# Second spectral layer: ways back through DRAM tiles of their own, one reload moved ahead of the last store, unread products moved

## The chip, the core and the metric

The kernel runs on one core of one Trainium2 chip. TensorE (PE) multiplies, VectorE (DVE), ScalarE (ACT) and GpSimd (POOL) work on the results, and transfers are issued on the queues of SyncE (SP) and of ACT. The metric is device time in microseconds (us), the median of several runs. Lower is better.

## What is computed

Four layers follow each other on one image of 48 x 48 pixels with 768 channels: a transformer block, a spectral layer, a scan with a convolution, and a second spectral layer. Only the spectral layers (the second and the fourth of these) are touched. In short:

```
xs  = rfft2(x)                          # 48 x 25 modes, 768 channels
xs  = xs in 8 blocks of 96 channels
o1  = relu(xs @ w1 + b1)                # complex, per block
o2  = o1 @ w2 + b2                      # complex, per block
out = irfft2(softshrink(o2, 0.01)) + x
```

All of it is float32.

## The kernel before

The Fourier transform over the width is made first, row by row, and its result is kept in two DRAM tensors `yu[0]` and `yu[1]`, one for each half of the 768 channels, laid out as [row of the spectrum, pixel row, 384 channels]. `spectrum_mix` (L1598) then does the rest of the spectral work. It is called once for each spectral layer, as "f1" and as "f3". The profile cuts these names to `f`, so `f_x` is the tile `x_...` of either layer and `f_yt` a loaded piece of spectrum. Which layer a row belongs to is seen from its time: f1 starts near 2615 us, f3 near 3341 us.

**The pipeline of `spectrum_mix`.** Its items are (group of channel blocks, chunk of five columns of the spectrum, block). In f3 there are four groups of two blocks, five chunks and so 40 items; the loop makes 44 steps. In each step four stages work on four different items: `s_ifft_h` on the item four steps back (product `f_u`, L1682, then the sum `f_us` on DVE, L1684), `s_mlp2` on the one three steps back (products `f_z`, L1666 and L1667, then `f_cl` and `f_Z` on DVE), `s_mlp1` on the one before (products `f_o`, L1645 to L1647), and `s_fft_h` on the newest (product `f_x`, L1631, copied by ACT to `f_X` and summed by POOL to `f_Xs`). All products take their PSUM banks in turn from one pool of eight. `beside(step)` adds other work to a step.

**Unread products.** `keep_warm` (L128) makes products that nothing reads, in a fixed place of PE's order. `spectrum_mix` makes three ahead of its first step and two ahead of each of steps 1 and 2, all in one bank taken as `first` (L1693 to L1698; `f_first` in the profile). Twelve more stand at the very end of f3 (`f_warm`, L1922). One such product is two passes of 384 columns.

**The ways back in f3** (`afno_second`, L1824). When both blocks of a chunk of a group are through, `put` (L1875) stores `us` to the same columns of `yu` from which it was loaded (L1877, 360 KB). The rows come back as `gts[group]`, a tile of 128 partitions: spectrum rows on partitions 0 to 49 for one half of the pixel rows and on 64 to 113 for the other half. For groups 0 to 2 this is done in six reloads of 50 rows by eight pixel rows, after the last chunk's store (L1882). For the last group each chunk of ten rows is reloaded by itself in two transfers of 180 KB, one for each half: chunks 0, 1 and 2 right behind their own stores, chunk 3 (the last but one) together with chunk 4 after the store of chunk 4. All of the last group's transfers are kept in program order. They are on SP's queue, but for one half of chunk 4, which is on ACT's queue. A reload must wait until the store of its chunk has landed, and SP's queue waits with it.

**The end.** `back` (L1900) makes the transform back over the width (product `f_w`, L1906), adds it to `x` on ACT and DVE in turn (L64, L66), and stores the output in pieces of 144 or 288 KB (L1896). For groups 0 to 2 it runs beside later steps; for the last group it runs after the twelve unread products.

The lines that decide the order of the last group's transfers:

```
elif group == final and kc != NKC - 2:
    for k in (kc,) if kc < NKC - 1 else (kc - 1, kc):
        for b in range(2):
            reload(nc.scalar if k == NKC - 1 and b else nc.sync, b, chunk(k), 0, G // 2)
```

Of the kernel before, what the change touches and what calls it, by code (L numbers as in the profile page):

```python
# [12 lines left out]
F32 = mybir.dt.float32  # L13
# [5 lines left out]
DRAM = bass.MemoryType.DRAM  # L19

P = 128
G = 48
# [4 lines left out]
NH, HD = 12, 64  # L27
# [16 lines left out]
NB, BS = 8, 96  # L44
KW = G // 2 + 1
KC = 5
KR = 2 * KW
NKC = KW // KC
# [79 lines left out]
def keep_warm(tc, ps, left, right, n):  # L128


    k, m = left.shape
    for _ in range(n):
        tc.keep_in_program_order(tc.nc.tensor.matmul(ps[:m, : right.shape[1]], lhsT=left, rhs=right, start=True, stop=True))
# [1428 lines left out]
def spectrum_open(tc, stack, name, a, layer, yu, side, groups, bufs):  # L1562


    nc = tc.nc
    w1, b1, w2, b2 = (a[f"{layer}_{k}"] for k in ("w1", "b1", "w2", "b2"))
    cp, yp = (stack.enter_context(tc.tile_pool(name=f"{name}_{n}", bufs=bufs, side=side)) for n, bufs in (("c", 1), ("y", bufs)))
    fh = cp.tile([BS, BS], F32, tag="fh", name=f"{name}_fh")
    nc.sync.dma_start(fh, a["fh"])
    w1t = cp.tile([BS, NB, 2, BS], F32, tag="w1", name=f"{name}_w1")  # L1570
    w1s, w1d = (cp.tile([BS, NB, BS], F32, tag=n, name=f"{name}_{n}") for n in ("w1s", "w1d"))
    w2t = cp.tile([BS + 1, NB, 2, BS], F32, tag="w2", name=f"{name}_w2")
    b1t = cp.tile([BS, 2, NB], F32, tag="b1", name=f"{name}_b1")
    ih = cp.tile([BS, BS], F32, tag="ih", name=f"{name}_ih")
    nc.sync.dma_start(w1t, w1)
    nc.sync.dma_start(b1t, b1)
    nc.sync.dma_start(w2t[:BS], w2)
    nc.sync.dma_start(w2t[BS : BS + 1], b2)
    nc.sync.dma_start(ih, a["ih"])
    nc.gpsimd.tensor_tensor(w1s, w1t[:, :, 0, :], w1t[:, :, 1, :], ALU.add)  # L1580
    nc.gpsimd.tensor_tensor(w1d, w1t[:, :, 1, :], w1t[:, :, 0, :], ALU.subtract)
    yts = {}

    def load(group, kc):
        if (group, kc) not in yts:
# [12 lines left out]
def spectrum_mix(tc, name, opened, psum, side, groups, put, beside):  # L1598

# [6 lines left out]
    nc = tc.nc  # L1606
    HB = NB // 2
    (fh, w1t, w1s, w1d, w2t, b1t, ih), load = opened
    with tc.tile_pool(name=f"{name}_s", bufs=2, side=side) as sp:
# [83 lines left out]
        warm = psum("first")  # L1693
        unread = lambda n: keep_warm(tc, warm, fh, w1t[:, :2].rearrange("p n r c -> p (n r c)"), n)
        unread(3)
        for step in range(len(items) + 4):
            if 0 < step < 3:
# [126 lines left out]
def afno_second(tc, a, scan, yu):  # L1824

    nc = tc.nc  # L1830
    ev = Evac(nc)
    out = a["out"].rearrange("(p s w) c -> s w p c", s=2, w=G)
    x3, scan_psum = next(scan)
    with ExitStack() as stack:
        GB = 2
        groups = [(n * GB // (NB // 2), n * GB % (NB // 2), GB) for n in range(NB // GB)]
        opened = spectrum_open(tc, stack, "f3", a, "L3", yu, "right", groups, 5)
        gp = stack.enter_context(tc.tile_pool(name="f3_g", bufs=1, side="right"))
        fw = by_rows(nc, gp, a["fw"], G, "fw")
        iw = by_rows(nc, gp, a["iw"], KR, "iw")  # L1840
        ready = [(half, g) for half in range(2) for g in range(NTB)]

        def rows_in(n, psum):
            half, g = ready[n]
            spectrum_rows(nc, fw, x3[:, 4 * g : 4 * g + 4, half * TB : (half + 1) * TB], yu, half, g, psum, gp, ev, "f3")
            if NTB <= n < NTB + 4:
                opened[1](0, n - NTB)


        for n, _ in enumerate(scan):  # L1850
            if n and n % 2 == 0:
# [10 lines left out]
        W = GB * BS  # L1862
        x3p = x3.rearrange("p (j b) c -> p b j c", b=2)

        def channels(group):
            half, b0, _ = groups[group]
            return slice(half * TB + b0 * BS, half * TB + b0 * BS + W)

        final = len(groups) - 1

        def put(group, kc, us, cols):
            half, b0, _ = groups[group]
            if cols.stop < W:
                return
            cs = slice(b0 * BS, b0 * BS + W)  # L1875
            pin = tc.keep_in_program_order if group == final else lambda ins: ins
            pin(nc.sync.dma_start(spectrum_of(yu[half], kc, cs), us))  # L1877
            if kc == 0:
                gts[group] = bp.tile([P, G // 2, W], F32, tag="gt", name=f"f3_gt_{group}")

            def reload(queue, b, rows, r0, n):
                pin(queue.dma_start(gts[group][b * HD + rows.start : b * HD + rows.stop, r0 : r0 + n], yu[half][rows, b * (G // 2) + r0 : b * (G // 2) + r0 + n, cs]))  # L1882

            chunk = lambda k: slice(2 * KC * k, 2 * KC * (k + 1))
            if group < final and kc == NKC - 1:
                for r0 in range(0, G // 2, 8):
                    for b in range(2):
                        reload(nc.sync, b, slice(0, KR), r0, 8)
            elif group == final and kc != NKC - 2:
                for k in (kc,) if kc < NKC - 1 else (kc - 1, kc):  # L1890
                    for b in range(2):
                        reload(nc.scalar if k == NKC - 1 and b else nc.sync, b, chunk(k), 0, G // 2)

        def store(queue, prs, cols):
            for s in range(2):
                queue.dma_start(out[s, :, prs, cols], x3[s * HD : s * HD + G, prs, cols])  # L1896

        def back(group, c):
            cols = channels(group)
            gt = gts[group].rearrange("p (j s) c -> p s j c", s=2)  # L1900
            for j in range(2):
                ps = [psum(f"w_{group}_{c}_{j}_{b}") for b in range(2)]
                for b in range(2):
                    keep = slice(b * HD, b * HD + KR)
                    for s in range(2):
                        nc.tensor.matmul(ps[b][s * HD : (s + 1) * HD, : 2 * W], lhsT=iw[keep], rhs=gt[keep, s, 4 * c + 2 * j : 4 * c + 2 * j + 2, :], start=True, stop=True)  # L1906
                for b in range(2):
                    ev(x3p[:, b, 4 * c + 2 * j : 4 * c + 2 * j + 2, cols], ps[b][: HD + G, : 2 * W].rearrange("p (j c) -> p j c", j=2))
                if group == len(groups) - 1:
                    store((nc.scalar, nc.sync)[j], slice(8 * c + 4 * j, 8 * c + 4 * j + 4), cols)  # L1910
            if group < len(groups) - 1:
                store(nc.scalar, slice(8 * c, 8 * c + 8), cols)

        each = NKC * GB
        backs = {each * (q + 1) + 8 + (2 if q < final - 1 else 1) * c: (q, c) for q in range(final) for c in range(3)}

        def beside(step):
            if step in backs:
                back(*backs[step])

        spectrum_mix(tc, "f3", opened, psum, "left", groups, put, beside)
# [111 lines left out]
```

## Time and profile before

| what | us |
|---|---|
| median of 3 runs | 3575.01 (3571.93 to 3576.77) |
| the profiled execution: its own time | 3578.66 |
| its span | 3576.8 |
| PE busy | 3513.7 (98%) |
| DVE, ACT, POOL busy | 2004.7, 1141.4, 680.8 |
| f_first: PE passes in the whole program, and longest | 28 of up to 0.53 |
| the 20 stores of `us` in f3, 360 KB each | issued from 3363 to 3551 |

The chain of waits is the work that ended last, followed back from the last instruction: what each piece waited for, or the piece before it on its engine. A line gives its start, its length and what it was. "issue" is time in which the engine waited for nothing that the profile shows. In lines of a timeline, the bracket at the end tells how long the engine stood idle before and what ended this. "SPq" and "ACTq" are the instructions that issue transfers on the queues of SP and ACT; merged lines include the waits between them. `f_gt<-yu` is a reload, `yu<-f_us` a store of a chunk, `f_yt<-yu` the load of a chunk, `out_dram<-x` a store of the output. In a table of stretches the columns are: length, busy time and instructions of PE, of the weight loads, of DVE, ACT and POOL, the clock granted to TensorE, the mean busy share of 16 DMA engines, and GB/s.

### The profile page before, as it was taken

Reading aid. Unit: us, or ns where it says so; the run is one execution under the profiler, and the core shown is the slowest. Engines: PE = TensorE matmul, PEld = TensorE weight load, DVE = VectorE, ACT = ScalarE, POOL = GpSimd, SP = SyncE. Lnnn points to the kernel's source line nnn. Section 1 sums busy time; section 2 is a strip of 40 time slices with the busy share of each in tenths; the row PEclk is TensorE's granted clock in tenths of the full one; section 3 lists DMA queues with packets and bytes.
Section 4 is the critical chain, followed back from the end, with each engine's and each line's share of the span. In section 5 each row is a group of like instructions: output and inputs, shape, how many; then the busy total and the mean of one; then the engine's idle time right before and its main releaser. Section 6 shows DMA issues by size and latency. Waiting matters only on the chain.

```text
span 3576.8 us, 52953 instructions
## 1 busy us (share of the span) xinstructions
PE 3513.7 (98%) x21274; PEld 2148.0 (60%) x21274; DVE 2004.7 (56%) x3015; ACT 1141.4 (32%) x1735; POOL 680.8 (19%) x572
## 2 busy tenths in 40 slices
PE   9999999999999999989999999999999998999998
PEld 5666554444444444555555555555578767996685
DVE  7644466766676776654234324232345578996554
ACT  1321254555555555203101210121023265223332
POOL 3211102111111110250000000000023303981121
PEclk9999999999999999999999999999999999999999
DMA  7555556655545443344346334533554403104456
GB/s 276 201 187 189 187 156 173 187 145 152 164 123 148 125 125 87 111 150 139 106 131 184 114 110 126 164 112 112 156 134 119 109 21 105 34 27 100 107 143 132
DMA packets 281171, 480.38 MB, mean 134 GB/s; under 512 B 37250, under 2 KB 234466, under 8 KB 274708
## 3 DMA queue, kind: packets, MB, share of 16 engines
q1 hardware_dynamic: 265322, 455.95, 43.8%
q10 hardware_dynamic: 15594, 20.94, 2.0%
q8 instruction: 171, 2.80, 0.3%
q14 instruction: 84, 0.69, 0.1%
HBM read 330.82 MB, written 145.98 MB: 133 GB/s over the span
## 4 chain that ended last, share of the span: by engine, by line
PE 91%; DVE 3%; POOL 2%; DMA 2%; ACT 1%; issue 1%; SPq 0%; ACTq 0%; DVEq 0%; POOLq 0%
PE p L996 14%; PE p L1059 13%; PE s L657 12%; PE av L688 12%; PE qk L375 6%; PE c L1223 4%; PE s L667 3%; PE c L1323 3%; PE v L180 3%; PE pj L180 3%; PE f_u L1682 2%; PE f_z L1666 2%; PE f_z L1667 2%; PE so L1410 2%; PE f_x L1631 2%; POOL t L1331 1%
## 5 line engine op out<-in xcount | busy, mean ns | idle before, releaser
L677 DVE TENSOR_TENSOR acc<-acc,p 128x928 f32<-128x928 f32 (+1 forms) x480 | 560.2, 1167 | 263.6 <-ACT p L669 222.6
L669 ACT ACTIVATE p<-s 128x928 f32<-128x928 f32 (+1 forms) x540 | 506.5, 940 | 491.6 <-PE s L667 470.0
L657 PE MATMUL s<-qt,kv 64*128 64x464 f32 (+1 forms) x2160 | 521.9, 559 | 7.5 <-DMA qt<-q_d 5.5
L1059 PE MATMUL p<-w,h 128*128 128x384 f32 x1512 | 492.3, 486 | 0.0
L688 PE MATMUL av<-p,kv 128*64 128x464 f32 (+1 forms) x2160 | 442.9, 554 | 0.0
L1059 PEld LDWEIGHTS p<-w,h 128*128 128x128 f32 x1512 | 285.6, 190 | 199.0 <-issue 4.2
L667 PE MATMUL s<-bt,oneh 64*128 64x464 f32 (+1 forms) x1080 | 400.8, 731 | 0.7 <-DMA bt<-rh_d 0.7
L688 PEld LDWEIGHTS av<-p,kv 128*64 128x64 f32 x2160 | 147.0, 137 | 261.9 <-issue 249.6
L657 PEld LDWEIGHTS s<-qt,kv 64*128 64x128 f32 x2160 | 203.0, 187 | 164.7 <-issue 153.4
L996 PE MATMUL p<-x2nT,w 128*128 128x384 f32 x864 | 294.0, 491 | 4.0 <-POOL rr L1035 4.0
L1323 PE MATMUL c<-H,bands 128*48 128x96 f32 x5632 | 245.1, 247 | 10.2 <-DVE th L1261 8.3
L375 PE MATMUL qk<-xnT,wqk 128*128 128x384 f32 x756 | 249.8, 487 | 0.3 <-DMA wqk<-wqk_d 0.3
L1323 PEld LDWEIGHTS c<-H,bands 128*48 128x48 f32 x5632 | 235.2, 124 | 20.3 <-issue 8.7
L996 PEld LDWEIGHTS p<-x2nT,w 128*128 128x128 f32 x864 | 165.2, 192 | 121.3 <-POOL rr L1035 4.2
L996 PE MATMUL p<-xT,w 128*128 128x384 f32 x648 | 220.8, 486 | 0.0
L1035 POOL TENSOR_TENSOR rr<-rr,ml_b 128x1152 f32<-128x1152 f32 x12 | 31.8, 2653 | 946.1 <-DMA rr<-xr_d 855.1
L991 ACT ACTIVATE h<-h,ml_b 128x384 f32<-128x384 f32 x144 | 88.5, 616 | 346.7 <-DVE h L1011 173.5
L375 PEld LDWEIGHTS qk<-xnT,wqk 128*128 128x128 f32 x756 | 141.4, 190 | 93.4 <-issue 0.9
L1331 POOL TENSOR_TENSOR t<-s,c 128x768 f32<-128x768 f32 x80 | 144.4, 1829 | 179.4 <-DVE s L1294 166.5
L996 PEld LDWEIGHTS p<-xT,w 128*128 128x128 f32 x648 | 123.1, 190 | 85.9
L667 PEld LDWEIGHTS s<-bt,oneh 64*128 64x128 f32 x1080 | 106.9, 188 | 105.7 <-issue 102.9
L1666 PE MATMUL f_z<-f_w,f_o 97*96 97x96 f32 x800 | 134.1, 249 | 0.0
(336 smaller groups left out, 4601.2 us busy)
## 6 DMA issues: line engine op xcount, KB each, us to landing
w<-w1s_d SPq DMA_DIRECT2D x36, 768.0 KB
w<-w2s_d SPq DMA_DIRECT2D x36, 768.0 KB
w<-w1s_d SPq DMA_DIRECT2D x36, 576.0 KB
w<-in_mlp_w_dram SPq DMA_DIRECT2D x27, 768.0 KB
yu<-f_ys SPq DMA_DIRECT2D x48, 384.0 KB
wqk<-wqk_d SPq DMA_DIRECT2D x12, 1344.0 KB
bt<-rw_d SPq DMA_DIRECT2D x72, 174.0 KB
bt<-rh_d SPq DMA_DIRECT2D x72, 174.0 KB
```

The lines of the kernel that those rows point to most:

```text
L180: nc.tensor.matmul(p[:, :TB], lhsT=rhs[n][:, c, t * P : (t + 1) * P], rhs=w[:, c, :], start=c == 0, stop=c == NC2 - 1)
L375: nc.tensor.matmul(p[:, :TB], lhsT=w[:, n, c, :], rhs=ops[sb][n][:, c, :], start=c == 0, stop=c == NC2 - 1)
L657: nc.tensor.matmul(ps[:, s, :n], lhsT=keys[pr % 2][rows, kt * P : (kt + 1) * P], rhs=held(c)[rows, :n], start=True, stop=False)
L667: nc.tensor.matmul(ps[:, s, :n], lhsT=oneh[rows, b % 2, :], rhs=bts[b // 2][rows, j, :n], start=False, stop=True)
L669: nc.scalar.activation(p, ps[:, :, :n], AF.Exp)
L677: nc.vector.tensor_tensor(probs[c], probs[c], p, ALU.add)
L688: nc.tensor.matmul(avs[c][rows, : size(c)], lhsT=vals[pr % 2][:, kt, rows], rhs=p[:, s, :], start=kt == 0, stop=kt == NT - 1)
L996: nc.tensor.matmul(p[:, :TB], lhsT=w[n][:, c, :], rhs=rhs[n][:, c, :], start=c == 0, stop=c == NC2 - 1)
L1059: nc.tensor.matmul(ps[t][:, :TB], lhsT=hs[left, f][:, t * P : (t + 1) * P], rhs=wt[:, f % KW2, :], start=f == 0, stop=f == NF2 - 1)
L1323: nc.tensor.matmul(ps[r0 : r0 + G, k // 4, cols], lhsT=bands[:, n - GC, i, :] if gr else bands0[:, n, i, :], rhs=H[:, n, :, d : d + NPR], ...
L1331: GP.tensor_tensor(t, sc[:, ch], c1[:, m0 : m0 + GC].unsqueeze(2).to_broadcast([P, GC, RR, NPR]), ALU.mult)
L1666: nc.tensor.matmul(out, lhsT=o1[:, j, 1:3, :].rearrange("c r h -> c (r h)"), rhs=w2t[:, b, 0, :], start=True, stop=False)
```

## The change

- The last stage of f3 gets DRAM tiles of its own, one for each group: [50 rows of the spectrum, 48 pixel rows, 192 channels]. `put` stores a chunk there and reloads it from there, and no longer goes through `yu`. In such a tile the pixel rows of one spectrum row, with all their channels, are one run of memory.
- For the last group every chunk is reloaded right behind its own store. Chunk 3 (the last but one) is therefore reloaded ahead of the store of chunk 4 on SP's queue.
- `spectrum_mix` no longer makes three unread products ahead of the first step, in either layer. In f3, which passes `alone=True`, it makes two ahead of each of the last two steps, 42 and 43. Each batch takes a bank of its own from the pool.

```
--- before.py
+++ after.py
@@ -1595,7 +1595,7 @@
     return yu[2 * KC * kc : 2 * KC * (kc + 1), :, cols].rearrange("(k r) p c -> (r p) k c", r=2)
 
 
-def spectrum_mix(tc, name, opened, psum, side, groups, put, beside):
+def spectrum_mix(tc, name, opened, psum, side, groups, put, beside, alone=False):
 
 
 
@@ -1690,11 +1690,9 @@
         items = [(g, kc, b) for g, (_, _, n) in enumerate(groups) for kc in range(NKC) for b in range(n)]
 
         stages = {s_ifft_h: 4, s_mlp2: 3, s_mlp1: 1, s_fft_h: 0}
-        warm = psum("first")
-        unread = lambda n: keep_warm(tc, warm, fh, w1t[:, :2].rearrange("p n r c -> p (n r c)"), n)
-        unread(3)
+        unread = lambda n: keep_warm(tc, psum(f"unread_{step}"), fh, w1t[:, :2].rearrange("p n r c -> p (n r c)"), n)
         for step in range(len(items) + 4):
-            if 0 < step < 3:
+            if 0 < step < 3 or alone and step > len(items) + 1:
                 unread(2)
             for stage, behind in stages.items():
                 if 0 <= step - behind < len(items):
@@ -1860,6 +1858,8 @@
 
         gts = {}
         W = GB * BS
+        dp = stack.enter_context(tc.tile_pool(name="f3_d", bufs=1, space=DRAM))
+        backs_d = [dp.tile([KR, G, W], F32, tag=f"yb{n}", name=f"yb{n}") for n in range(len(groups))]
         x3p = x3.rearrange("p (j b) c -> p b j c", b=2)
 
         def channels(group):
@@ -1869,27 +1869,24 @@
         final = len(groups) - 1
 
         def put(group, kc, us, cols):
-            half, b0, _ = groups[group]
             if cols.stop < W:
                 return
-            cs = slice(b0 * BS, b0 * BS + W)
             pin = tc.keep_in_program_order if group == final else lambda ins: ins
-            pin(nc.sync.dma_start(spectrum_of(yu[half], kc, cs), us))
+            pin(nc.sync.dma_start(spectrum_of(backs_d[group], kc, slice(0, W)), us))
             if kc == 0:
                 gts[group] = bp.tile([P, G // 2, W], F32, tag="gt", name=f"f3_gt_{group}")
 
             def reload(queue, b, rows, r0, n):
-                pin(queue.dma_start(gts[group][b * HD + rows.start : b * HD + rows.stop, r0 : r0 + n], yu[half][rows, b * (G // 2) + r0 : b * (G // 2) + r0 + n, cs]))
+                pin(queue.dma_start(gts[group][b * HD + rows.start : b * HD + rows.stop, r0 : r0 + n], backs_d[group][rows, b * (G // 2) + r0 : b * (G // 2) + r0 + n, :]))
 
             chunk = lambda k: slice(2 * KC * k, 2 * KC * (k + 1))
             if group < final and kc == NKC - 1:
                 for r0 in range(0, G // 2, 8):
                     for b in range(2):
                         reload(nc.sync, b, slice(0, KR), r0, 8)
-            elif group == final and kc != NKC - 2:
-                for k in (kc,) if kc < NKC - 1 else (kc - 1, kc):
-                    for b in range(2):
-                        reload(nc.scalar if k == NKC - 1 and b else nc.sync, b, chunk(k), 0, G // 2)
+            elif group == final:
+                for b in range(2):
+                    reload(nc.scalar if kc == NKC - 1 and b else nc.sync, b, chunk(kc), 0, G // 2)
 
         def store(queue, prs, cols):
             for s in range(2):
@@ -1918,7 +1915,7 @@
             if step in backs:
                 back(*backs[step])
 
-        spectrum_mix(tc, "f3", opened, psum, "left", groups, put, beside)
+        spectrum_mix(tc, "f3", opened, psum, "left", groups, put, beside, True)
         keep_warm(tc, psum("warm"), opened[0][0], opened[0][1][:, :2].rearrange("p n r c -> p (n r c)"), 12)
         for c in range(3):
             back(final, c)
```

More of the change, by code (lines that the diff above doesn't have):

```diff
@@ L1595, in spectrum_of, with spectrum_mix @@
     return yu[2 * KC * kc : 2 * KC * (kc + 1), :, cols].rearrange("(k r) p c -> (r p) k c", r=2)
-def spectrum_mix(tc, name, opened, psum, side, groups, put, beside):
+def spectrum_mix(tc, name, opened, psum, side, groups, put, beside, alone=False):
     nc = tc.nc
@@ L1692, in spectrum_mix @@
         stages = {s_ifft_h: 4, s_mlp2: 3, s_mlp1: 1, s_fft_h: 0}
-        warm = psum("first")
-        unread = lambda n: keep_warm(tc, warm, fh, w1t[:, :2].rearrange("p n r c -> p (n r c)"), n)
-        unread(3)
+        unread = lambda n: keep_warm(tc, psum(f"unread_{step}"), fh, w1t[:, :2].rearrange("p n r c -> p (n r c)"), n)
         for step in range(len(items) + 4):
-            if 0 < step < 3:
+            if 0 < step < 3 or alone and step > len(items) + 1:
                 unread(2)
@@ L1862, in afno_second @@
         W = GB * BS
+        dp = stack.enter_context(tc.tile_pool(name="f3_d", bufs=1, space=DRAM))
+        backs_d = [dp.tile([KR, G, W], F32, tag=f"yb{n}", name=f"yb{n}") for n in range(len(groups))]
         x3p = x3.rearrange("p (j b) c -> p b j c", b=2)
@@ L1871, in put @@
         def put(group, kc, us, cols):
-            half, b0, _ = groups[group]
             if cols.stop < W:
                 return
-            cs = slice(b0 * BS, b0 * BS + W)
             pin = tc.keep_in_program_order if group == final else lambda ins: ins
-            pin(nc.sync.dma_start(spectrum_of(yu[half], kc, cs), us))
+            pin(nc.sync.dma_start(spectrum_of(backs_d[group], kc, slice(0, W)), us))
             if kc == 0:
@@ L1881, in reload @@
             def reload(queue, b, rows, r0, n):
-                pin(queue.dma_start(gts[group][b * HD + rows.start : b * HD + rows.stop, r0 : r0 + n], yu[half][rows, b * (G // 2) + r0 : b * (G // 2) + r0 + n, cs]))
+                pin(queue.dma_start(gts[group][b * HD + rows.start : b * HD + rows.stop, r0 : r0 + n], backs_d[group][rows, b * (G // 2) + r0 : b * (G // 2) + r0 + n, :]))
             chunk = lambda k: slice(2 * KC * k, 2 * KC * (k + 1))
@@ L1888, in put @@
                         reload(nc.sync, b, slice(0, KR), r0, 8)
[L1889 to L1892, printed above, removed]
+            elif group == final:
+                for b in range(2):
+                    reload(nc.scalar if kc == NKC - 1 and b else nc.sync, b, chunk(kc), 0, G // 2)
         def store(queue, prs, cols):
@@ L1919, in beside @@
                 back(*backs[step])
-        spectrum_mix(tc, "f3", opened, psum, "left", groups, put, beside)
+        spectrum_mix(tc, "f3", opened, psum, "left", groups, put, beside, True)
         keep_warm(tc, psum("warm"), opened[0][0], opened[0][1][:, :2].rearrange("p n r c -> p (n r c)"), 12)
```

## The prediction

> **What bounds the kernel now.** I read the page's first part, then the chain of waits over the last 240 us and the last 40 us, SP's queue in the same time, and the table of 1 us stretches.
>
> TensorE (PE) is nearly always busy. From 3357 to 3542 us the chain of the second spectral layer is PE alone, in steps of 4.57 us (6.2 with a way back in them), so what is changed beside those steps costs nothing. Only where PE waits can the change pay. The stage's start:
>
> ```profile
> PE 3513.7 (98%) x21274; PEld 2148.0 (60%) x21274; DVE 2004.7 (56%) x3015; ACT 1141.4 (32%) x1735; POOL 680.8 (19%) x572
> ...
> 3339.97 1.27 issue
> 3341.24 2.15 PE f_first L133 x6
> 3343.39 0.86 PE f_x L1631 x10
> ```
>
> Three unread products (six passes) stand between the wait for a bank and the first real product, f_x. The first spectral layer starts likewise:
>
> ```profile
> 2615.24 2.15 PE L133 MATMUL f_first<-f_w,f_fh 96*96 96x384 f32 x6 [0.74 <-DVE rr L1039]
> 2617.22 1.01 PE L1631 MATMUL f_x<-f_fh,f_yt 96*96 96x96 f32 x10
> ```
>
> The end:
>
> ```profile
> 3543.88 1.25 PE f_u L1682 x2
> 3545.13 0.32 PE f_z L1666 x2
> ...
> 3550.72 0.67 DVE f_us L1684
> ...
> 3551.40 3.70 DMA yu<-f_us
> ...
> 3555.12 7.88 DMA f_gt<-yu
> ...
> 3563.25 6.99 PE f_w L1906 x46
> ```
>
> A store, a reload and the products back follow each other with nothing beside them. A pair of f_z passes takes 0.32 us where all steps before show 0.17: the clock is halved. The stretches (last three columns: clock, DMA share, GB/s) say so too, and show a reload at 91 GB/s, the last stores at 262:
>
> ```profile
> 3545.00:3546.00 1.00, 1.00 (x8) 1.00 (x7) 0.00 (x0) 0.00 (x0) 0.00 (x0) 0.50 1.10 200
> 3559.00:3560.00 1.00, 0.00 (x0) 0.00 (x0) 0.00 (x0) 0.00 (x0) 0.00 (x0) 1.00 0.75 91
> 3573.00:3574.00 1.00, 0.00 (x0) 0.00 (x0) 0.00 (x0) 0.00 (x0) 0.00 (x0) 0.50 0.90 262
> ```
>
> SP's queue (chunks of the final group counted 0 to 4): chunk 2 is reloaded at 3540.28, chunk 3 stored at 3541.37, chunk 4 at 3551.40, and only then come the reloads of 3 and 4:
>
> ```profile
> 3540.28 0.69 SPq L1882 DMA_DIRECT2D f_gt<-yu  x2
> 3541.37 10.34 SPq L1877 DMA_DIRECT2D yu<-f_us  x2
> 3551.80 3.59 SPq L1882 DMA_DIRECT2D f_gt<-yu  x3
> ```
>
> The landing events give the ends: store 3 at 3548.07; reload of chunk 3, half 0, at 3557.84, half 1 at 3560.29; of chunk 4 at 3563.00 and 3563.70.
>
> [...] the last three halves landed 2.45 and 2.71 us apart (chunks 0 to 2: 1.9 to 2.1). [...] the trace shows ten separate landing events for such a reload, sixteen for a store. [...] it is 0.50 from 3544.8 to 3548.2 after a wait of 1.53 us; after the wait of 1.43 at 3548.2 it is not.
>
> **The change, part by part** (own time of the profiled execution 3578.66, span 3576.8).
>
> *Three unread products less, second layer.* f_x waits for the same bank and its data landed long ago: it moves from its start at 3343.22 to f_first's, 3341.24. Gain 2.0. Nothing else comes late: the first product's copies need ACT and POOL, which are idle.
>
> *The same, first layer.* There f_x needs its first load, whose last landing event is at 2616.55, not 2617.22: 0.6 at most. But PE then waits from 2614.5 to 2616.6, 2.1 us; if the clock halves, f_x (0.85) and what it overlaps run at half speed, and the first f_o, which stands at 2619.69, starts at about 2616.6 + 1.7 + 1.7 (copy and sum) + 0.3 = 2620.3, a loss of 0.6. I take 0; both ends go into the range.
>
> *A bank of its own per batch of unread products.* The eight-bank ring is moved by one; the readers of the reused banks were done over 1.5 us before. 0.
>
> *Two products ahead of each of the last two f_u.* Four passes of 0.32 us are 1.3 us, inside the waits of 1.53 and 1.43. They hold the clock: f_z's last batch takes 1.87 instead of 3.30 us, f_u a little less, so us is complete 1.6 us earlier, and the store of chunk 4 can start at 3549.8. Cost if the cover were gone: 2.6.
>
> *Contiguous DRAM tiles.* Stores keep runs of 768 B. Reloads of groups 0 to 2 (50 rows) get runs of 6144 B, of the final group 18,432 B. Such runs do get joined: the layer's way-in stores show packets of 6144 B. This shortens the 5.9 us in which SP issues six reloads, beside PE's steps: 0 on the path. For the final group it changes the packets[...]: I take 2.71 us a half as before. Bounds: nothing, or 1.4 us a half (a packet of 18,432 B elsewhere took 0.71, two per engine) if packets are the limit.
>
> *Chunk 3 reloaded ahead of store 4.* On SP the store of chunk 4 is now queued behind the wait for store 3 (3548.07) and two issues (0.7): free at 3548.9, before 3549.8, so the wait itself costs 0. Store 3 may land a little earlier, as the whole of SP's queue moved up: I take 3547 (bounds 3545 and 3549.7). But on the ten engines the packets of reload 3 now stand ahead of store 4's. That order is in the trace: the reload of chunk 0 was issued at 3521.77, its halves landed at 3526.97 and 3529.10, and store 1, queued behind it, at 3529.64: 7.9 us after the reload's issue. Store 4 then lands at 3547.1 + 7.9 = 3555.0, against 3555.1 now. Next the reload of chunk 4, alone: 1.0 us to the first packet (as from 3551.40 to 3552.4), two halves one after the other at 2.5 each, 0.3 to land: 6.3, so 3561.3, against 3563.70. Gain 2.4. It contains the 1.6 above: us is early, but the queue is late next. If halves 0 and 1, on SP's and ACT's queues[...], run side by side, 2.5 more.
>
> *The products back* still start about 4 us after the 24 warm passes end (3558.4 - 1.6), so the clock is halved again, and the last stores run at 220 to 260 GB/s whatever comes before: 0. If the reload landed within a microsecond of the warm passes, 48 passes would take 4.4 instead of 7 us, and the stores start some 1.1 us earlier.
>
> Sum: 2.0 + 0 + 2.4 = 4.4 us, so 3574.3 beside 3578.66. The runs' median, 3575.01, lies 3.65 below the profiled execution; [...] some of them need not have the halved f_z (1.6), and there the gain is smaller. I take 0.4 off: 4.0, **3571.0 us**.
>
> **Rivals.**
> *A. Packets[...] bind the reload, or its two halves overlap.* Reload 4 takes 3.8 us or less, store 4 lands near 3553.5, the last half at 3557.5, and the products run partly at full clock: 6.2 + 1.1 + 2.0 = 9.3, less 0.4: 3566. For: the tiles' rows become one run; two queues. Against: 50-row reloads of the same 768 B packets move at up to 211 GB/s, and reload halves stood 2.7 apart[...].
> *B. Only the start pays.* Store 4 stands so long behind reload 3 (landing at 3557, halves of 2.71) that reload 4 is no earlier: gain 2, 3573.
> *C. Slower: SP is held ahead of store 3.* Before store 2, SP waited 4.2 us for an output store to land, though its data was ready. If other transfers now fall together so, ahead of store 3 (3541.4), until the outputs of 3540.85 land (3549.7), store 3 lands at 3553, store 4 and reload 4 follow 8.0 + 6.3 later at 3567.3: 3.6 lost against 2.0 won, with the 0.6 in the first layer 2.2 net, 3577.2. It decides once store 3 lands after 3551.4 (3563.7 + 2.0 - 14.3).
> *D. No joined runs:* packets stay 768 B; the order and the start still act, as forecast, and so it is inside the forecast's case.
>
> **Numbers.** Forecast 0.5 (own range 3568 to 3573.5), A 0.27, B 0.16, C 0.07. The range reaches to A's and past B's time: 3564.5 to 3575.5, leaving out some of A below and C above. 0.2% of 3575 is 7.15 us, about what a measurement can tell: faster means below 3567.9. A's most and the forecast's lower edge: 0.29; C beyond 3582: 0.03; the rest 0.68.
>
> **What would show it.** f_first gone and f_x at 3341.2 less what came before; f_z pairs at 0.17 to the end; reload packets of 18,432 B; the last store's landing 3 to 7 us after its issue; reload halves 2.5 us apart or together. I'm wrong if they land together, or if store 3 lands much before 3545 or after 3551.

## The result, and the profile after

The changed kernel took 3568.58 us in the median of 12 runs (3565.89 to 3575.88), the kernel before 3575.21 us (12 runs, 3571.93 to 3579.33). The ratio is 0.9984, 95% interval 0.9976 to 0.9992: a gain of 2.9 to 8.6 us. The forecast was 3571.0 us.

Together with these, the three sets of runs below hold 54 runs of the changed kernel and 165 of the kernel before. Their means are 3570.21 and 3575.25 us. The standard deviations, divided by the root of the number of runs, make these means uncertain by 0.5 and 0.2. So the change is worth **5.0 us, give or take 0.5**. The forecast's sum was 4.4, less 0.4: 4.0.

The two profiled executions differ by 12.7 us in span (3576.8 and 3564.1), more than the change is worth (the one after was the fastest of its twelve runs), so the first question is where. From marks that both traces have ("third f_o" is the first f_o product of the third item):

| stretch | before, us | after, us | gain |
|---|---|---|---|
| start to the last MLP product ahead of the first spectral layer | 2614.50 | 2607.11 | 7.4 |
| from there to the third f_o of that layer | 14.23 | 13.70 | 0.5 |
| from there to the last way-in product of the second | 710.7 | 710.9 | -0.1 |
| from there to the second layer's third f_o | 15.21 | 14.55 | 0.7 |
| from there to the last f_x | 177.21 | 177.21 | 0 |
| from the last f_x to the end | 44.93 | 40.65 | 4.3 |

The first line stands ahead of everything that the diff touches, so it is not the change's; the same mark moved by up to 7.6 us over the profiles of all kernels here, which share that code. What the change did is in the lines below it.

What answers to the lines shown of before is, first, the chain at the second spectral layer's start (start, length, what):

```profile
3332.21 1.27 issue
3333.48 1.06 PE f_x L1631 x10
3334.54 2.17 PE f_unread L133 x4
3336.71 0.80 PE f_o L1645 x2
```

The three products are gone and f_x follows the wait for a bank. But the four passes of unread products now take 2.17 us, where six took 2.15 before, and f_x 1.06 against 0.86. One stretch of 1 us shows why (last columns: clock, DMA share, GB/s):

```profile
3336.00:3337.00 1.00, 1.00 (x4) 0.60 (x3) 0.00 (x0) 0.00 (x0) 0.00 (x0) 0.50 0.98 252
```

The clock is halved there, from 3334.8 to 3338.2 us, 3.4 us long; before it was 1.00 at this place (3341 to 3346). The first layer's start, on PE's timeline:

```profile
2604.69 2.42 PE L1059 MATMUL p<-w,h 128*128 128x384 f32 x7
2609.28 1.06 PE L1631 MATMUL f_x<-f_fh,f_yt 96*96 96x96 f32 x10 [2.17 <-DMA f_yt<-yu]
2611.79 0.65 PE L1645 MATMUL f_o<-f_Xs,f_w 96*96 96x240 f32 x2 [0.16 <-POOL f_Xs L1635]
```

PE waits 2.17 us for the load, as the forecast said, and this time keeps its clock (1.00 from 2607 to 2613). The chain of the end:

```profile
3538.00 0.18 PE f_z L1667 x2
...
3539.60 1.06 PE f_u L1682 x2
...
3540.68 0.67 DVE f_us L1684
...
3541.37 3.93 DMA yb<-f_us
...
3545.36 6.21 DMA f_gt<-yb
...
3551.71 4.10 PE f_w L1903 x44
```

f_z pairs stay at 0.17 us up to the last, the last store leaves 1.6 us earlier (17.92 us after the last f_x began, 19.53 before), its landing takes about as long as before (3.93 and 3.70), the reload 6.21 instead of 7.88, and the products back 4.10 instead of 6.99. SP's queue in that time:

```profile
3532.95 0.32 SPq L1875 DMA_DIRECT2D yb<-f_us  x1
3538.40 0.65 SPq L1880 DMA_DIRECT2D f_gt<-yb  x2
3541.37 0.32 SPq L1875 DMA_DIRECT2D yb<-f_us  x1
3545.32 0.27 SPq L1880 DMA_DIRECT2D f_gt<-yb  x1
3554.65 5.56 SPq L1893 DMA_DIRECT2D out_dram<-x  x6
```

Store 3, reload 3, store 4, reload 4: the new order. SP was free 2.3 us ahead of store 4. And the queues' totals in packets (then MB and share):

```profile
q1 hardware_dynamic: 256952, 455.95, 43.4%
q10 hardware_dynamic: 15364, 20.94, 2.0%
```

On q1 8370 packets are gone, on q10 230, with the same bytes. 18 reloads of groups 0 to 2 fell from 400 packets to 50 each (6300), ten of the final group from 240 to 10 each (2300, one of them on ACT's queue): together 8600, every one. The runs of memory are joined into longer packets, as forecast.

### The profile page after: what moved, and what is told of

The parts are those of the page before. It is cut to its first block, busy times and chain, and to the rows that moved or that the text cites. A ratio compares the mean times of both kernels' runs of the same rounds, so it can differ in the third digit from the quotient of the medians.

```text
span 3564.1 us, 52947 instructions
## 1 busy us (share of the span) xinstructions
PE 3507.8 (98%) x21270; PEld 2145.7 (60%) x21270; DVE 2002.1 (56%) x3015; ACT 1140.5 (32%) x1735; POOL 677.3 (19%) x572
## 4 chain that ended last, share of the span: by engine, by line
PE 90%; DVE 4%; DMA 3%; POOL 2%; ACT 1%; issue 1%; SPq 0%; ACTq 0%; DVEq 0%; POOLq 0%
PE p L996 14%; PE p L1059 13%; PE s L657 12%; PE av L688 12%; PE qk L375 6%; PE c L1223 4%; PE s L667 3%; PE c L1323 3%; PE v L180 3%; PE pj L180 2%; PE f_u L1682 2%; PE f_z L1667 2%; PE f_z L1666 2%; PE so L1410 2%; PE f_x L1631 2%; PE f_o L1645 1%
```

## The experiments

All times in the next table are from the start of the last f_x. S is the landing of a chunk's store (its last landing event), R3 and R4 are the reloads of chunks 3 and 4 (second half's landing), "tail" is the time to the span's end.

| kernel | S3 | R3 issued | S4 | R4 | tail |
|---|---|---|---|---|---|
| before | 17.29 | 19.93 | 23.23 | 31.83 | 44.93 |
| after | 14.94 | 14.95 | 21.85 | 28.13 | 40.65 |
| after, second (e8) | 15.77 | 15.79 | 22.83 | 29.11 | 42.19 |
| after, third (e11) | 16.55 | 16.57 | 23.48 | 29.71 | 42.61 |
| e1, shared `yu` | 16.97 | 16.99 | 24.15 | 29.95 | 42.95 |
| e2, old order | 15.83 | 18.34 | 21.43 | 29.51 | 42.70 |
| e3, no end products | 18.50 | 18.51 | 25.53 | 31.78 | 44.82 |
| e4, e10, tail only | 16.13, 16.49 | 16.15, 16.51 | 22.99, 23.55 | 29.31, 30.03 | 42.45, 42.74 |
| e5, rows spread | 14.49 | 14.51 | 20.85 | 25.60 | 38.36 |
| e6, products back in the first layer | 15.98 | 16.00 | 22.85 | 29.37 | 42.34 |
| e7, products back in the second layer | 17.13 | 17.14 | 23.90 | 30.12 | 43.04 |
| e9, start only | 18.88 | 19.93 | 22.89 | 31.84 | 45.09 |

Theory 1 is the forecast's: order pays, the last reload keeps its time whatever the length of its packets, tiles and end products are worth nothing. Each experiment names its rival. Each time below stands beside the kernel before of its own set (3575.45 us for e1 to e4, 3574.55 for e5 to e8, 3575.91 for e9 to e11); means are compared with 3575.25 and 3570.21, and "±" gives one standard error. The kernel before itself averaged 3575.5, 3574.6 and 3575.9 in the three sets, and the changed kernel did not run in the first of them, so differences of about 1 us between kernels of different sets are not read.

### e1: the tiles undone

The order and the products stay, and the ways back go through `yu` again.

```
+            half, b0, _ = groups[group]
+            cs = slice(b0 * BS, b0 * BS + W)
...
-            pin(nc.sync.dma_start(spectrum_of(backs_d[group], kc, slice(0, W)), us))
+            pin(nc.sync.dma_start(spectrum_of(yu[half], kc, cs), us))
...
-                pin(queue.dma_start(gts[group][b * HD + rows.start : b * HD + rows.stop, r0 : r0 + n], backs_d[group][rows, b * (G // 2) + r0 : b * (G // 2) + r0 + n, :]))
+                pin(queue.dma_start(gts[group][b * HD + rows.start : b * HD + rows.stop, r0 : r0 + n], yu[half][rows, b * (G // 2) + r0 : b * (G // 2) + r0 + n, cs]))
```

> The changed kernel, but stores and reloads go through the shared yu again (runs of 768 B), with the new order and the products at the end kept. The measure is the tail, from the start of the last forward product f_x to the end of the span: 44.9 us before, 40.7 after; and the last reload of chunk 4, from its issue to its second landing: 7.9 us before, 6.2 after. Theory 1 ([...] the tiles add nothing on the path): reload 6.0 to 6.6, tail 40 to 41.5. Rival (the long runs of the own tiles made the reload quicker): reload 7 to 8, tail 42.5 to 44, and most of the gain in time gone.

Measured: 3572.18 us, ratio 0.9990 (0.9982 to 0.9998). With packets of 768 B the last reload took 5.80 us from S4 to R4, against 6.28 with packets of 18,432 B in the changed kernel. Long runs do not speed it. Its halves landed 0.67 us apart, with long runs 1.79 (1.4 to 2.0 in every kernel with long runs and ten neighbouring rows). In the changed kernel each half was ten packets, and each packet of the second half (begun from 3547.11 to 3548.67) began where one of the first ended (from 3547.10 to 3548.67). The tail, 42.95, is longer than theory 1 wanted and lies where the rival had it, though not by the rival's way: the reload was not slower, but S3 landed at 16.97, just above what the changed kernel shows by itself in three profiles (14.94 to 16.55). The mean, 3571.51, is 1.3 ± 1.0 above the changed kernel's.

The tiles do move something ahead of S3. SP's queue at the six reloads of the group before and at the first store of the last group, in the kernel before and then in the changed one:

```profile
3507.05 6.10 SPq L1882 DMA_DIRECT2D f_gt<-yu  x6
3513.25 1.90 SPq L1877 DMA_DIRECT2D yu<-f_us  x1
```

```profile
3498.53 2.48 SPq L1880 DMA_DIRECT2D f_gt<-yb  x6
3501.51 0.32 SPq L1875 DMA_DIRECT2D yb<-f_us  x1
```

With tiles the six reloads take 2.48 us to issue and not 6.10, and that store goes out as soon as its data is there, 21.9 us ahead of the last f_x in all ten kernels with tiles; in the three that go through `yu` (before, e1, e9) it goes out 18.5 to 18.7 us ahead of it. The next store lands 3.7 to 6.5 us ahead of the last f_x with tiles, 2.0 to 2.7 through `yu`. S3 itself lies at 14.5 to 18.5 with tiles and at 17.0 to 18.9 through `yu`. So the tiles may have a part in the gain at the end, by way of S3; that they do is not shown.

### e2: the old order of the last two chunks

```
-            elif group == final:
-                for b in range(2):
-                    reload(nc.scalar if kc == NKC - 1 and b else nc.sync, b, chunk(kc), 0, G // 2)
+            elif group == final and kc != NKC - 2:
+                for k in (kc,) if kc < NKC - 1 else (kc - 1, kc):
+                    for b in range(2):
+                        reload(nc.scalar if k == NKC - 1 and b else nc.sync, b, chunk(k), 0, G // 2)
```

> The changed kernel, with chunk 3 reloaded behind the store of chunk 4 as before; own tiles and the products at the end kept. Theory 1: reload 4 queues behind reload 3 again, 7.5 to 8 us from the landing of store 4; the products at the end still bring store 4 forward by 1.6 us; the products back find a halved clock: tail 43 to 43.6. Rival (long runs move quickly, the order is nothing): all four halves land within 5 us of the store, tail 40 to 41.

Measured: 3569.05 us, ratio 0.9983 (0.9975 to 0.9991); mean 3569.28, not above the changed kernel's. SP's queue shows the order back:

```profile
3533.60 8.74 SPq L1875 DMA_DIRECT2D yb<-f_us  x2
3542.44 3.38 SPq L1880 DMA_DIRECT2D f_gt<-yb  x3
```

The tail, 42.70, is a little shorter than the 43 to 43.6 of theory 1. R4 lands 8.08 us after S4 (before: 8.60), because two reloads share that time; in the new order it is 6.28. Yet R4 lands at 29.51, between the changed kernel's 28.13 and 29.71. The reason is in S4. With the old order no reload stands between stores 3 and 4 on SP's queue, so the 1.6 us that the end products give reach its landing (21.43 against 23.23). With the new order S4 follows R3's issue instead: it came 6.8 to 7.2 us after it, in all kernels with ten neighbouring rows, whether store 4 was issued 0.7 or 3.0 us after it. In the changed kernel's trace the packets of reload 3 ended from 3540.16 to 3543.55, and those of store 4, issued at 3541.37, ran from 3542.21 to 3544.88. So of the 2.3 us that R4 gained here (31.83 to 29.51) 1.8 were there at S4, without the new order. This reads as if **the order and the end products were substitutes**, both together giving little more than either. It is argued from single profiles and not shown in time: no kernel here has the tiles and the shorter starts and neither of the two, and the times of e2 and e3 alone would fit as well if neither paid.

### e3: no unread products at the end

```
-        spectrum_mix(tc, "f3", opened, psum, "left", groups, put, beside, True)
+        spectrum_mix(tc, "f3", opened, psum, "left", groups, put, beside)
```

> The changed kernel without the two unread products ahead of each of steps 42 and 43. If the clock halves there, as it did in the profile of the kernel before (f_z passes at 0.16), the store of chunk 4 is issued 1.6 us later. Theory 1 (the store lands behind reload 3[...] anyway): about 1 us of it shows, tail 41.3 to 42.2. Rival (the products are the whole gain): tail 43 or more. Where the clock does not halve in this execution, the tail is that of the changed kernel, 40.7, in both.

Measured: 3568.69 us, ratio 0.9983 (0.9976 to 0.9990); mean 3569.35, again not above the changed kernel's. With the new order no worth of the end products shows in time, as the forecast had it. The profile can't tell whether a late store 4 would be hidden: the clock did not halve in it ahead of the last products, and `us` was complete at 17.89, as with the end products, and not at 19.50 as in the profiles of before and e9. Yet its tail is long, 44.82, where theory 1 had 40.7 without a halved clock, and its queue tells why:

```profile
3532.57 1.05 SPq L1880 DMA_DIRECT2D f_gt<-yb  x2
3533.72 1.00 SPq L1875 DMA_DIRECT2D yb<-f_us  x1
3541.09 0.65 SPq L1880 DMA_DIRECT2D f_gt<-yb  x2
3541.83 0.32 SPq L1875 DMA_DIRECT2D yb<-f_us  x1
3548.13 0.27 SPq L1880 DMA_DIRECT2D f_gt<-yb  x1
```

Reload 2, the first line, went out 10.0 us after the last f_x began (5.6 in the changed kernel), since store 2 landed that late; store 3 stood behind it on SP's queue, so it was issued 1.6 us later than in the changed kernel, and landed at 18.50. Store 4 was ready at 3540.5 and was held: SP issued it at 3541.83. This is the forecast's rival C, short of the point from which it costs more than it wins. One execution came that near; the 19 runs say it isn't the rule. (In e9's profile, with the old order, store 2 was as late and S3 came at 18.88.)

### e4, e6 and e7: the three first products back in both layers, in the first, in the second

```
-            if 0 < step < 3 or alone and step > len(items) + 1:
-                unread(2)
+            if step < 3 or alone and step > len(items) + 1:
+                unread(2 if step else 3)
```

This is e4. In e6 two lines are added instead, here in one: `if not step and not alone: unread(3)`; in e7 `if not step and alone: unread(3)`.

> The changed kernel with three unread products ahead of the first step again, in both layers. The measure is the time from the end of the last way-in product to the second f_o batch of the second layer: 10.7 us before, 10.1 after (where the clock was halved for 3.4 us after the wait of 1.8). Theory 1 (the three products stand on the path): 10.7 at full clock, 2.0 more than the changed kernel at full clock would need (8.7). Rival (they hold the clock and pay for themselves): the changed kernel and this one come out equal, within 0.7, because the clock halves without them. First layer, from the last product of the MLP to the first f_o: 5.2 us before, 4.7 after; here 5.2.

> The changed kernel with the three products ahead of the first step kept in the first spectral layer only. Theory 1 (the first load's landing ends the wait there anyway): 0.5 us slower than the changed kernel at the first f_o, nothing else. Rival (what is won in the first layer grows behind it): 3 us or more, which would explain the 5.7 us by which the median with both was above the changed kernel's.

> The changed kernel with the three products kept in the second spectral layer only. Theory 1: 2.0 us slower at full clock, 0.7 where the clock halves after the wait of 1.8 us; median 1 to 2 us above the changed kernel. Rival (the second layer's start is worth more than its products, since all transfers of the last group follow it): 4 us or more.

Measured: e4 3574.26 us, ratio 0.9996 (0.9987 to 1.0004); e6 3569.01, 0.9987 (0.9981 to 0.9994); e7 3570.88, 0.9990 (0.9983 to 0.9996). Means: e6 3569.99, as the changed kernel; e7 3570.89, 0.7 ± 0.6 above it. So the first layer's products are worth nothing that shows (0.6 would not show either), the second's perhaps 0.7. But e4, which only does both edits at once, stood 5.7 us above the changed kernel's first median. Two parts worth 0 and 0.7 don't make 5.7, and its trace has no place for it: its start is the one of before (15.20 us to the third f_o), its tail, 42.45, is that of the changed kernel. Hence the next two sets.

### e8 and e11: the changed kernel again

> The changed kernel once more, for a second profile and to see how far its time moves by itself. Theory 1: reload 3 is issued when store 3 has landed, store 4 lands 6.9 to 7.2 us after that issue, and the last reload 6.2 to 6.4 after store 4, so the last landing is 13.2 us after store 3's, whatever store 3's is (14.4 to 18.5 us after the last f_x so far); tail 40.6 to 43. Rival (the steps vary by themselves): the sum of 13.2 does not hold. Median 3567 to 3571.

> The changed kernel unaltered, a third time, so that the two halves above have the whole beside them on the same chip. Theory 1: 4 to 6.5 us below the kernel before. Its profile shows how far the landing of the store of chunk 3 and the clock in the products back move from one execution to the next: landing 14.4 to 18.5 us after the last forward product began, last reload 13.2 after that.

Measured: 3569.37 us, ratio 0.9986 (0.9980 to 0.9993), and 3569.84, 0.9984 (0.9978 to 0.9991). The whole is steady over three sets. What moves the end is seen in the third execution's chain:

```profile
3545.01 5.55 DMA yb<-f_us
3550.63 6.17 DMA f_gt<-yb
3556.94 7.43 PE f_w L1903 x44
```

The reload takes what it took before (6.17 and 6.21). The last store takes 5.55 us instead of 3.93, since S3 and so R3's issue came 1.6 later. And the products back take 7.43 instead of 4.10: PE had waited longer (3.29 us ahead of the first f_w, 1.64 in the changed kernel's first profile), and the clock was halved (0.50 in the stretch from 3558 to 3559).

### e9 and e10: only the start, only the end

e9 is the kernel before without one line; e10 is e4 again.

```
-        unread(3)
```

> The kernel before, without the three unread products ahead of the first step of either layer; nothing else of the change. Theory 1 (the gain is the sum of what the trace shows at its places: 0.4 to 1.0 us at the first layer's start, 0.7 to 2.0 at the second's, about 2.5 at the end): 1.1 to 3.0 us below the kernel before, so 3572 to 3574; the end as before, with the last reload landing 15 to 16 us after the landing of the store of chunk 3 and the tail near 45 us. Theory 2 (what the runs of the three-first kernel said: the end is worth 1 us and the starts the rest): 5 us or more below the kernel before.

> The changed kernel with the three unread products back ahead of the first step of both layers, so only the end of the change is left; the same kernel as the three-first one, run again. Theory 1: 2.0 to 3.0 us below the kernel before, and 1 to 3 above the changed kernel; together with the start-only kernel the two gains make up the whole. Theory 2: again no more than 1.2 below the kernel before. If the two gains sum to less than the whole change's by over 2 us, either they help each other or the medians move by that much.

Measured: e9 3575.61 us, ratio 0.9996 (0.9988 to 1.0005), mean 3574.31; e10 3573.22 us, ratio 0.9994 (0.9986 to 1.0002). With e4's runs e10's kernel has 26, mean 3573.46. So the start alone gains 0.9 ± 1.0 us and the end alone 1.8 ± 0.5 (against the kernel before of each one's own set: 1.6 ± 1.1 and 2.2 ± 0.5). e10's kernel is 3.2 ± 0.7 above the changed one, so part of e4's 5.7 was chance. The 15 to 16 us that the expectation had from store 3 to the last reload rest on a wrong landing of store 3 (see below); they were 14.5 in the kernel before and 13.0 here. Theory 2 of these two (the starts carry 5 us) falls. e10's timeline shows one thing more:

```profile
3333.39 3.20 PE L133 MATMUL f_unread<-f_w,f_fh 96*96 96x384 f32 x6 [1.78 <-issue]
3336.38 1.66 PE L1631 MATMUL f_x<-f_fh,f_yt 96*96 96x96 f32 x10
```

Here the six passes took 3.20 us and f_x 1.66, at a clock of 0.50 (the stretch from 3336 to 3337): it can be halved *with* the three products too.

### e5: the ten rows of a chunk spread over the partitions

The final group's rows go to every fifth partition instead of ten neighbours; the matrix of the transform back is loaded once more with its rows in the same order. Theory 1 is here that the reload's time hangs on the partitions on which its rows land. Its 1.4 us a half is the author's estimate, half of the 2.71 us that lie between two landings of halves in the kernel before.

```
+        iws = bp.tile([P, iw.shape[1]], F32, tag="iws", name="f3_iws", bufs=1)
+        for k in range(NKC):
+            for b in range(2):
+                nc.sync.dma_start(iws[b * HD + k : b * HD + KR : NKC], a["iw"][2 * KC * k : 2 * KC * (k + 1)])
...
-                    reload(nc.scalar if kc == NKC - 1 and b else nc.sync, b, chunk(kc), 0, G // 2)
+                    queue = nc.scalar if kc == NKC - 1 and b else nc.sync
+                    pin(queue.dma_start(gts[group][b * HD + kc : b * HD + KR : NKC], backs_d[group][chunk(kc), b * (G // 2) : (b + 1) * (G // 2), :]))
...
-                        nc.tensor.matmul(ps[b][s * HD : (s + 1) * HD, : 2 * W], lhsT=iw[keep], rhs=gt[keep, s, 4 * c + 2 * j : 4 * c + 2 * j + 2, :], start=True, stop=True)
+                        nc.tensor.matmul(ps[b][s * HD : (s + 1) * HD, : 2 * W], lhsT=(iws if group == final else iw)[keep], rhs=gt[keep, s, 4 * c + 2 * j : 4 * c + 2 * j + 2, :], start=True, stop=True)
```

> The changed kernel, but the ten rows of each chunk of the last group come back to every fifth partition and not to ten neighbours, with the rows of the last transform's matrix in the same order. [...] Theory 1[...]: two halves of 1.4 us and not of 2 to 2.7, so store 4 lands at most 5.5 us after reload 3's issue and the last reload takes 3.8 to 4.6 us and not 6.2 to 6.4; tail 38 to 39.5. Rival (packets or the ten engines bind it): reload 6 us or more, tail 40.5 to 42.5.

Measured: **3565.64 us**, ratio 0.9975 (0.9967 to 0.9984), mean 3565.67: 9 us below the kernel before and 4.5 ± 0.8 below the changed one, the best of all kernels here. The same bytes in the same packets of 18,432 B took 4.75 us from S4 to R4 instead of 6.28, R3 took 4.61 from its issue instead of 6.35, and the halves of the last reload landed 0.99 apart instead of 1.79. A packet of its second half took 2.0 us in the changed kernel and 0.9 here. So the partitions on which the rows land did bind the reload, for 1.5 of its 6.28 us. Two of the expectation's figures, the author's estimates, were missed: 4.6 for the reload by a little, and store 4, which came 6.3 us after R3's issue and not 5.5, as it was only issued 3.4 us after it. PE's timeline and SP's queue show the rest:

```profile
3538.61 7.90 PE L133 MATMUL f_warm<-f_w,f_fh 96*96 96x384 f32 x24
3546.45 4.96 PE L1908 MATMUL f_w<-f_gt,f_iws 50*64 50x384 f32 x48
```

```profile
3536.09 1.47 SPq L1894 DMA_DIRECT2D f_gt<-yb  x2
3539.50 0.31 SPq L1879 DMA_DIRECT2D yb<-f_us  x1
3542.45 0.72 SPq L1894 DMA_DIRECT2D f_gt<-yb  x1
```

The store of chunk 4 lands 2.93 us after its issue, and the products back follow the twelve warm products with no wait and a full clock (48 passes in 4.96 us, 6.98 before). The tail is 38.4 us.

## Why the prediction was right, and where it was not

**The time.** 3571.0 was forecast; 3568.58 was the first median, 3570.2 the mean of all runs, inside the forecast's own case. Rival A's time, 3566, is about as near to that first median, but its mechanism isn't what happened: the halves did not run side by side, and R4 took 6.3 us, not 3.8. Rival B needed S4 two microseconds later than before; in the three profiles of the changed kernel it came between 1.4 earlier and 0.3 later. Rival C's mechanism was seen once with the new order (e3, S3 at 18.50), short of its point: 3551.4 us in before's time is 19.5 in the table. Rival D is out by the count of packets.

**Second layer's start: 2.0 forecast.** f_x came 1.98 earlier after the last way-in product (1.79 us, before 3.77). The step had a gap: "nothing else comes late" left out the clock, which it had considered for the first layer alone. After the wait of 1.78 us it was halved in seven of the nine profiles without the products (for 3.4 us in the changed kernel's; the four unread passes took 1.94 to 2.77 us in the seven, 1.46 in e3 and e5), and there only 0.66 of the 1.98 was left at the third f_o. It is no pure loss of the change, since with the products the clock halved in two profiles of four (e7 and e10, where six passes took 2.78 and 3.20 us; 2.15 in before and e4). At equal clock the gain is what was forecast: 15.20 to 13.27 (not halved, e4 and e3), 16.85 to 14.55 (halved, e10 and after). The means over the profiles of each kind, 15.96 and 14.26, give 1.7. The clock was halved or not after the same wait of 1.78 us; what decides it is not shown. At the end of the kernel before it was 0.50 from 3544.5 to 3547.9 us, behind a wait of 1.53, and 1.00 behind the wait of 1.43 at 3548.2. That in some executions f_z is not halved there, for which the forecast took 0.4 off, was the author's estimate; e3's profile is one, with waits of 1.53 and 1.43 us.

**First layer: 0, within 0.6.** f_x does wait for its load. The third f_o came 14.2 us after the last MLP product with the three products, and 13.2 to 13.7 without, in all profiles but one: e8, where the clock halved after the wait of 2.09 us (four unread passes in 2.05 us, 1.46 in the changed kernel), had 14.92, the loss of about 0.6 that the step named. On average 0.6 is gained, the step's upper end. In time e6 is 0.2 ± 0.9 below the changed kernel, which can't show 0.6 either way.

**End products: absorbed.** Nothing speaks against it: `us` was 1.6 earlier than in the two profiles in which the clock halved without them (before, e9), and without them the new order loses no time (e3 is 0.9 ± 0.8 below the changed kernel). A late store 4 behind reload 3 was not seen. What the step did not see is that the 1.6 reach S4 in the old order (e2).

**Tiles: 0 on the path.** For the last reload this was right: its packets did not matter (6.2 to 6.5 us in eight profiles with long runs, 5.80 in e1). But the step put at nothing that SP issues the six reloads sooner, while the step on the order let store 3 land earlier because SP's queue moved up. What that is worth is open (e1, 1.3 ± 1.0).

**The order: 2.4.** The sum came out about right, in part by luck, and three of its terms were off. The landing of store 3 was misread: 3548.07 is where the first of the two output stores of 3540.85 landed. The semaphore on which SP waits ahead of reload 3 has its last landing event at 3549.16, the 17.29 of the table. So to take store 3 at 3547 meant 2.2 us earlier, not 1.1, and it came: in the changed profile it was 3546.8 (3531.87, where the last f_x began before, and 14.94), in the two others 3547.6 and 3548.4. Store 4 was to land 7.9 us after reload 3's issue; it took 6.8 to 7.2 in all kernels of the new order with neighbouring rows, so this term was 0.9 too large. The last reload was to take 6.3, and took 6.28; but of its parts 1.0 to the first packet with 2.5 a half was not right: the first half landed after 4.49 us and the second 1.79 later. Together R4 follows S3 by 13.0 to 13.5 us in every such kernel, where 14.3 was forecast. With before's own S3 of 17.29 that makes 30.3 to 30.8 against 31.83: the order by itself is worth 1.0 to 1.5 there, and the rest of what R4 gained (3.7 in the profile shown, 2.7 and 2.1 in the two others) came from S3 being earlier. In the old order R4 does not hang on S3: it was 31.83 and 31.84 with S3 at 17.29 and 18.88 (before, e9). So the order pays only as far as S3 is early; at 18.88 it would by this sum have won nothing. S3 moves between 14.5 and 18.9, and it follows the landing of store 2 by 8.0 to 9.5 us in all thirteen profiles. So what moves it lies ahead of store 2 (the six reloads, the output stores of the group before); beyond e1, that was not tried.

The reload's time was half right. The prediction took 2.71 us a half whatever the packets, which is what lay between the landings at 3560.29 and 3563.00 before, and the time did not fall with long packets. Which partitions the rows land on has a part in it, as e5 shows. Two halves of 1.36 us, half of 2.71 (the author's estimate for spread rows), would save 2.7 us; measured were 1.5 of 6.3. So where the ten rows lie cost 1.5 here. What makes up the other 4.75 is not shown.

**The products back: 0.** This was right in most profiles, and in the one shown it wasn't: R4 at 28.13 came 3.2 us after the warm products, the clock stayed full (1.00 from 3338.2 to 3560.1), and f_w took 4.10 instead of 6.99, where it was halved from 3561.6 to 3568.4. Of these 2.9 us only about 0.6 reached the end: the tail after R4 was 12.5 us (12.8 in e5, where the clock stayed full too), against 12.7 to 13.3 where the clock was halved for all of it or a part. The output stores take their time whatever f_w does: from the first's issue to the end 10.6 us before and 10.9 after, at 261 GB/s:

```profile
3553.00:3554.00 1.00, 1.00 (x17) 0.55 (x13) 0.82 (x3) 0.00 (x0) 0.00 (x0) 1.00 0.00 0
3558.00:3559.00 1.00, 0.00 (x0) 0.00 (x0) 0.00 (x0) 0.00 (x0) 0.00 (x0) 1.00 0.90 261
```

**The account.** By the traces: first layer 0.6, second layer's start 1.7, tail 2.7 (45.0 over the two profiles with the old end, before and e9, 42.3 over the seven with the new). That is 5.0, against 5.0 ± 0.5 measured; that they agree so closely is luck, as the seven tails lie between 40.65 and 43.04.

**What stays open.** The start alone (0.9 ± 1.0) and the end alone (1.8 ± 0.5) sum to 2.7 ± 1.1, and the whole is 5.0 ± 0.5. The gap of 2.3 is about twice its own uncertainty. Against the kernel before of each one's own set the parts sum to 3.8 ± 1.2, and the gap is 1.2 ± 1.3. So it is not shown that the parts help each other. Two things were not tried: tiles, shorter starts and neither order nor end products, which would tell whether these two are substitutes; and the tiles alone, which would tell what they do to S3.

## What to carry to other kernels

When several edits shorten one chain of store, reload and products, look which wait each one ends: two that feed the same point may be worth no more than one of them, and taking out either alone, as in e2 and e3, can then show nothing. Look, too, on which partitions a reload of few rows lands; here to spread the rows was worth 4.5 us on top of the change, nearly as much as the change itself. A landing must be read from the semaphore on which the next instruction waits; here the neighbour's was 1.1 us off. And a difference between two profiled executions must be cut at marks ahead of the edit before it is read, as 7.4 of 12.7 us here were not the change's.

## What the hardware showed that was not expected

- The clock. The changed kernel's runs with a mean granted clock of 0.993 averaged 3572.6 us (18 runs), with 0.994 3568.9 (25), with 0.995 3566.8 (7), with 0.992 3573.3 (4). So part of the movement between runs of one kernel goes with the clock, and not most of it: runs with the same figure still scatter with a standard deviation of 2.6 us, all 54 together with 3.4.
- The clock was halved for 3.4 us behind a wait of 1.53 us in the kernel before and one of 1.78 in the changed one, and stayed at 1.00 behind one of 2.17 us in the changed kernel's first layer. In e8 a wait of 2.09 at that place was enough (four passes in 2.05 us instead of 1.46).
- Packets 24 times as long did not shorten a ten-row reload (6.28 us with 18,432 B in the changed kernel, 5.80 with 768 B in e1), and with them the two queues' halves landed 1.79 us apart instead of 0.67.
